# The end of part 1 in another order, and the one-hot of the low rank digits from 16-bit operands

## The chip, the cores and the metric

The kernel runs on one core of a Trainium2 chip. The core has a matrix engine (TensorE, PE in the profile), three engines for element-wise work (VectorE or DVE, ScalarE or ACT, GpSimd or POOL), a synchronisation engine (SyncE or SP) that here only issues DMAs, and 16 DMA engines that move data between the memory outside the core (HBM) and the memory on it (SBUF). Each engine executes its own instructions in a fixed order and waits where an input or a buffer is not ready; an instruction behind a waiting one waits with it.

The metric is the device time of one execution in microseconds (us). It is given as the median of several runs. A profiled execution is a separate one, and it has its own time.

## What is computed

The kernel is one layer of graph attention. There are 3327 nodes with 1024 features, and a symmetric adjacency matrix of integers in which few entries of a row are one.

```python
h = jnp.maximum(_layernorm(x, axis=-1), 0.0)
f = h @ Wf + bf
g = h @ Wg + bg
e = jax.nn.relu(f @ g.T)
scores = jnp.where(adj > 0, e, NEG)
attention = jax.nn.softmax(scores, axis=1)
out = x + attention @ (h @ W + bW)
```

## The kernel before

The kernel doesn't compute the full matrix of scores. It finds the neighbours of each node and gathers only their rows of h. The nodes are held in NT = 26 tiles of 128 rows; the last tile has 127. The code is in `edge_path`, and it has two parts. (A dense way of computing the same stands behind a test at the end, and isn't executed with these inputs.)

**Part 1** makes four things: h, stored in HBM as the table `hd`; the list of neighbours of every row, stored as `pd` with the remaining candidates in `cd`; the matrix A = Wf Wg^T, so that one product per tile yields the vector q with which a row's scores are dot products of q and neighbours' rows of h; and `perm`, the order of all nodes by degree. Part 2 then handles nodes in groups of 128 nodes of like degree.

The main loop of part 1 runs over i from 0 to 22. For tile i+2, `degrees` (line 686, ACT, 691) turns the adjacency into 0 and 1 and adds each row up, and `keys` (695, POOL, 698) multiplies by column numbers, in two halves. For tile i, `segments` (756, DVE, 761) takes the eight largest keys in each of 16 segments, and `listed` (763, DVE, 768 to 776) makes the list out of these 128 candidates. Beside this run the layer norms. `load_x` (678) reads a tile of x. `measured` (700) takes mean and variance on DVE for an odd tile; for an even one, `rooted` (711) takes them with two passes on ACT, and for an odd one it is two short instructions. `inverted` (727, DVE) is a reciprocal, `scaled` (731, ACT) writes h in place, and `store_h` (737) stores it. The tables `at_load`, `at_stats` and `at_scale` (850 to 852) say in which i each tile has these steps. The stage of the loop also issues the load of adjacency tile i+5 (`load_adj`, 671), loads of Wf, and PE's products for A (`plan`). All DMAs of part 1 except three small or late ones go through SP's queue, in the order of the code.

Ranks by degree come from one-hot matrices: `one_hot` (782) makes `oh` from the degrees; `before` and `after` (791, 794) are PE products that add up prefixes; `placed` (797, DVE) reads the row's place off. After the loop comes the tail, lines 965 to 1120, for the last three tiles 23, 24 (`late`) and 25 (`last`). It completes prefix sums, computes `rank`, splits it in a low part of seven bits and a high part (`lo`, `hi`), makes a one-hot of each (`ohp`, line 1034, 3328 elements a partition; `ohs`, 1040), and PE multiplies the two in 26 products (1049). Their result, after three short steps, is `perm` (1057). Two gathers (1062) then fetch the rows of h for the first two groups, and PE computes their q in six products of a third each (1075). DVE meanwhile finishes the lists of tiles 23, 24 and 25 (1096 to 1106).

All of part 1 lies in a `manual_schedule`: each engine has its instructions in the order of the code. Buffers are taken in turn: six of 128 x 1024 for x (`ln`, `xt`), which also receive the two gathers, and five of 128 x 3327 for the adjacency (`kpool`, `r`), which also hold the work space and `ohp` of the tail. A load into a buffer waits for the last reader of what was in it. W is read by one DMA of POOL's queue (1064) into the buffer of Wg's transpose.

**Part 2** has 26 groups. For each, POOL issues gathers of the lists (L), of the group's own rows (H) and of the neighbours' rows (G) into 26 row buffers; PE turns the own rows and computes q; DVE takes a dot product for each neighbour (1222); ACT takes exponentials; the weighted rows are added up on DVE (1272) or PE (1260), and PE multiplies by W (1287). The whole order of instructions comes from `planned` (550), which works it out from assumed durations and start times; once built, it is fixed for each engine. One of its steps, `told` (1318), copies a flag from a PE result that stands behind the last of the six q products (1155); it has its place in DVE's order among the dots of the first group.

Of the kernel before, what the change touches and what calls it, by code (L numbers as in the profile page):

```python
# [10 lines left out]
FP = mybir.dt.float32  # L11
I32 = mybir.dt.int32
AF = mybir.ActivationFunctionType
ALU = mybir.AluOpType
# [7 lines left out]
BF = mybir.dt.bfloat16  # L22
SEG = 16
# [552 lines left out]
def edge_path(ctx: ExitStack, tc: tile.TileContext, x, adj, Wf, bf, Wg, bg, W, bW, out, flag):  # L576
# [11 lines left out]
    nc = tc.nc  # L588
    N, D = x.shape
# [54 lines left out]
    with ExitStack() as part1:  # L644
# [26 lines left out]
        def load_adj(t, parts=((0, N),)):  # L671
            n = rows(t)
            r = rs[t] = kpool.tile([P, N], FP, name="r")
            for c0, c1_ in parts:
                for b, m in pieces(t):
                    nc.sync.dma_start(r.bitcast(I32)[b : b + m, c0:c1_], adj[t * P + b : t * P + b + m, c0:c1_])

        def load_x(t):
            xt = xs[t] = ln.tile([P, D], FP, name="xt")
            for b, m in pieces(t):  # L680
                nc.sync.dma_start(xt[b : b + m], x[t * P + b : t * P + b + m, :])
# [45 lines left out]
        def inverted(t):  # L727
            rstd = stats[t][1]
            nc.vector.reciprocal(rstd[: rows(t)], rstd[: rows(t)])
# [76 lines left out]
        def empty():  # L806
            while emptied1:
                emptied1.pop(0)()
# [40 lines left out]

        at_load = {t: t + 2 for t in range(18)} | {18: 20, 19: 21, 20: 21, 21: 22, 22: 22, 23: 22, 24: 22}  # L850
        at_stats = {t: t + 4 for t in range(16)} | {16: 20, 17: 20, 18: 21, 19: 22, 20: 22}
        at_scale = {t: t + 5 for t in range(16)} | {16: 21, 17: 21, 18: 22}
        of = lambda table, i: [t for t in range(NT) if table.get(t) == i]

        with tc.manual_schedule(engines={
# [5 lines left out]
            for b, e in HALVES:  # L861
                nc.gpsimd.iota(
                    iotaj[:, b:e], pattern=[[1, e - b]], base=b + 1, channel_multiplier=0, allow_small_or_imprecise_dtypes=True
                )
            held = p_c.tile([P, NBIN + BATCH * KL + SEG * 8], FP, name="held")
            iotad, pos = held[:, :NBIN], held[:, NBIN + BATCH * KL :]
# [48 lines left out]
            for i in range(NT - 3):  # L915
                degrees(i + 2)
                keys(i + 2, nc.gpsimd)
                if i < 3:
                    for c in (2 * i + 2, 2 * i + 3):
                        transposed(WgT[:, :, c * P : (c + 1) * P], A_sb[:, c, :D])  # L920
                        empty()
# [15 lines left out]
                if i + 5 < NT:  # L937
                    load_adj(i + 5)
                for c in range(KD):
                    if wants[c] - 2 == i:  # L940
                        load_w(Wf, c)
# [21 lines left out]
                for t in of(at_load, i):  # L963
                    load_x(t) if t >= NT - 3 else None
            late, last = NT - 2, NT - 1
            degrees(last)
            keys(last, nc.gpsimd)
            empty()
            one_hot(late, last)
            one_hot(last, NT)  # L970
            for t in (NT - 7, NT - 6):
                inverted(t)
                scaled(t)
            store_left(NT - 4)
            store_h(NT - 7)
            load_x(last)
            store_h(NT - 6)
            measured(NT - 5, True)
            rooted(NT - 5)
            measured(NT - 4, False)  # L980
            rooted(NT - 4)

            s = 0
            after(counted - 1)
            for t in range(counted, NT):
                before(t)
                segments(NT - 3, s, s + 2)
                s += 2
                placed(t)
                after(t)  # L990
                if t == NT - 3:
                    for u in (NT - 5, NT - 4):
                        inverted(u)
                    for u in (NT - 5, NT - 4):
                        scaled(u)
                        store_h(u)
            segments(NT - 3, s, s + 1)
            measured(NT - 3, True)
            rooted(NT - 3)
            measured(late, False)  # L1000
            rooted(late)

            work = kpool.tile([P, N], FP, name="r")
# [7 lines left out]
            slots = slots.rearrange("p (t s) -> p t s", s=NT)  # L1011
            ohp = kpool.tile([P, N], FP, name="r").bitcast(BF)[:, : NT * P].rearrange("p (t d) -> p t d", d=P)

# [3 lines left out]
            nc.vector.tensor_mul(above, oh, incl[:, None, :].to_broadcast([P, NT, NBIN]))  # L1017
            inverted(NT - 3)
            scaled(NT - 3)
            store_h(NT - 3)  # L1020
            rank = c1.tile([P, NT], FP, name="rank")
            nc.vector.tensor_reduce(rank, above, AX.X, ALU.add)
            ranki = c1.tile([P, NT], I32, name="ranki")
            nc.vector.tensor_add(ranki, rank, rp)
            lo = c1.tile([P, NT], I32, name="lo")
            nc.vector.tensor_scalar(lo, ranki, P - 1, None, op0=ALU.bitwise_and)
            hi = c1.tile([P, NT], I32, name="hi")
            nc.vector.tensor_scalar(hi, ranki, 7, None, op0=ALU.logical_shift_right)
            inverted(late)
            scaled(late)  # L1030
            store_h(late)
            measured(last, True)
            rooted(last)
            nc.vector.tensor_tensor(
                ohp, lo[:, :, None].to_broadcast([P, NT, P]), iotap[:, None, :].to_broadcast([P, NT, P]), op=ALU.is_equal
            )
            inverted(last)
            scaled(last)
            store_h(last)
            nc.vector.tensor_tensor(  # L1040
# [3 lines left out]
                place[:, :, 0, :], ohs, iotap[:, :NT, None].to_broadcast([P, NT, NT]), op=ALU.mult  # L1044
            )
            nc.vector.tensor_scalar(place[:, :, 1, :], ohs, part, None, op0=ALU.mult)
            ps = p_mm.tile([P, CB], FP, name="ps_A")
            for t in range(NT):
                nc.tensor.matmul(
                    ps[:, : 2 * NT], ohp[:, t, :], place[:, t, :, :].rearrange("p a s -> p (a s)"),  # L1050
                    start=(t == 0), stop=(t == NT - 1),
                )
            segments(NT - 3, s + 1, SEG)
            tens = c1.tile([P, NT], FP, name="tens")
# [5 lines left out]
            for s in ORDER[:2]:  # L1060
                hps.append(ln.tile([P, D], FP, name="xt"))
                gather(hps[-1], hd[:, :], perm[:, s : s + 1])
            W_sb = wgpool.tile([P, KD, QW], FP, tag="wg", name="W_sb")[:, :, :O]
            nc.gpsimd.dma_start(W_sb, W.rearrange("(k p) o -> p k o", p=P))

# [29 lines left out]

            listed(NT - 3)
            store_lists(NT - 2 - BATCH, NT - 2)
# [274 lines left out]
```

## Time and profile before

| what | value |
|---|---|
| median of 3 runs | 1243.84 us (1241.71 to 1244.11) |
| the profiled execution's own time | 1279.55 us |
| its span | 1277.8 us |
| mean granted PE clock | 0.951 |
| DVE busy | 1134.0 us (89%) |
| PE busy | 1127.0 us (88%) |
| POOL busy | 876.2 us (69%) |
| ACT busy | 618.1 us (48%) |
| DMA | 374.46 MB, mean 293 GB/s |

The profile is of one execution, and its span is 36 us above the median of the runs; sums over its durations are to be set against its own time. The columns of a slice row are 40 equal parts of the span, and each digit is the busy share in tenths. In a timeline, the bracket behind an instruction says how long its engine sat idle before it and which instruction or DMA seems to have released it. The releaser is inferred; where an instruction awaits several things, it can be the wrong one.

In the stretch around the change the windows of the trace give:

| stretch, us | PE busy | DVE busy | ACT busy | POOL busy | DMA share | GB/s |
|---|---|---|---|---|---|---|
| 140 to 180 | 37.62 | 31.96 | 32.63 | 38.93 | 1.03 | 391 |
| 180 to 200 | 7.81 | 17.75 | 15.86 | 11.45 | 0.96 | 287 |
| 200 to 220 | 1.39 | 12.65 | 18.79 | 10.62 | 0.56 | 193 |
| 220 to 240 | 10.96 | 19.45 | 5.62 | 3.02 | 0.67 | 212 |
| 240 to 250 | 10.00 | 6.77 | 1.87 | 0.00 | 0.86 | 338 |
| 250 to 260 | 10.00 | 3.45 | 1.78 | 7.45 | 0.47 | 140 |
| 400 to 600 | 180.58 | 185.72 | 102.14 | 141.87 | 0.90 | 314 |

### The profile page before, as it was taken

How to read it: one execution, taken by the hardware profiler on the slowest of the kernel's cores; microseconds unless marked ns; L12 is line 12 of the kernel's file. 1: busy time of each engine (PE TensorE's matmuls, PEld its weight loads, DVE VectorE, ACT ScalarE, POOL GpSimd, SP SyncE). 2: the span in 40 equal slices, each digit the busy share in tenths (PEclk: the TensorE clock that was granted, in tenths of full speed). 3: DMA queues.
4: the chain of work that ended last, by engine and by line, in shares of the span. 5: the costliest groups of instructions: out<-in, count | busy, mean ns of one | idle time of the engine just before them, and what ended most of it. 6: DMA issues, size and time to landing. Idle time of an engine off the chain costs nothing. (4 is left out here: it accounts for less than half of the span.)

```text
span 1277.8 us, 14478 instructions
## 1 busy us (share of the span) xinstructions
PE 1127.0 (88%) x4632; PEld 720.7 (56%) x4632; DVE 1134.0 (89%) x2167; ACT 618.1 (48%) x941; POOL 876.2 (69%) x677
## 2 busy tenths in 40 slices
PE   2799980887987899997999799999999999999995
PEld 2566650555646467655766465665655665555553
DVE  6999977778798999999999979898999999999991
ACT  5899978234418256544644254453323433333250
POOL 8999975277576667677677657557676776766711
PEclk9899985798998999999999899999999999989998
DMA  9999996689768989989899879679987998989941
GB/s 369 418 379 397 404 347 233 209 313 340 268 204 298 340 274 328 313 311 311 284 325 293 305 221 332 216 259 330 311 299 236 339 270 305 271 291 296 321 110 52
DMA packets 101803, 374.46 MB, mean 293 GB/s; under 512 B 14747, under 2 KB 18490, under 8 KB 98519
## 3 DMA queue, kind: packets, MB, share of 16 engines
q0 software_dynamic: 80624, 290.96, 67.9%
q1 hardware_dynamic: 21094, 82.49, 17.1%
q8 instruction: 38, 0.62, 0.2%
q14 instruction: 47, 0.39, 0.1%
HBM read 344.11 MB, written 29.30 MB: 292 GB/s over the span
## 5 line engine op out<-in xcount | busy, mean ns | idle before, releaser
L635 POOL DMA_INDIRECT G<-hd,ps x454 | 524.3, 1155 | 243.6 <-issue 103.1
L1222 DVE CUSTOM_DVE_ANT_0 junk<-G,q 128x1024 bf16<-128x1024 f32 x468 | 601.6, 1286 | 40.0 <-DMA G<-hd,ps 28.7
L1209 PE MATMUL p_q<-A_sb,hT 128*128 128x342 f32 x1152 | 361.1, 463 | 14.7 <-ACT hT L1205 5.2
L1287 PE MATMUL p_o<-W_sb,yT 128*128 128x512 f32 x832 | 368.2, 598 | 3.7 <-ACT yT L1283 3.3
L1272 DVE SCALAR_TENSOR_TENSOR G<-G,sc 128x1024 f32<-128x1024 f32 x257 | 330.9, 1287 | 11.5 <-ACT G L1245 10.4
L1209 PEld LDWEIGHTS p_q<-A_sb,hT 128*128 128x128 f32 x1152 | 217.5, 195 | 124.0 <-issue 17.4
L1287 PEld LDWEIGHTS p_o<-W_sb,yT 128*128 128x128 f32 x832 | 158.2, 192 | 194.3 <-issue 184.7
L1260 PE MATMUL p_y<-ident,G 128*128 128x128 f32 x1688 | 208.2, 276 | 21.4 <-issue 11.5
L1260 PEld LDWEIGHTS p_y<-ident,G 128*128 128x128 f32 x1688 | 192.5, 143 | 53.5 <-issue 25.5
L1256 ACT ACTIVATE G<-G,sc 128x1024 f32<-128x1024 f32 x185 | 197.2, 1137 | 0.1
L698 POOL TENSOR_TENSOR r<-r,iotaj 128x1664 f32<-128x1664 f32 (+3 forms) x50 | 183.8, 3762 | 15.0 <-ACT r L691 15.0
L1298 ACT ACTIVATE xp<-p_o,rs 128x512 f32<-128x512 f32 x50 | 33.1, 682 | 213.1 <-DMA out_dram<-xp,perm 80.9
L831 PE MATMUL ps_A<-WgT,WfT 128*128 128x342 f32 x432 | 132.2, 465 | 2.4 <-ACT WfT L826 2.4
L761 DVE MAX8 cand<-r 128x8 f32<-128x208 f32 (+2 forms) x416 | 119.1, 360 | 4.0 <-POOL r L698 3.7
L831 PEld LDWEIGHTS ps_A<-WgT,WfT 128*128 128x128 f32 x432 | 82.5, 195 | 43.5 <-issue 3.3
L1215 ACT COPY q<-p_q 128x342 f32<-128x342 f32 x72 | 31.8, 445 | 128.0 <-PE p_q L1209 51.5
L691 ACT ACTIVATE r<-r 128x3327 f32<-128x3327 int32 (+3 forms) x27 | 77.3, 2862 | 8.1 <-DMA r<-in_adj_dram 8.1
L1283 ACT COPY yT<-p_y 128x512 f32<-128x512 f32 x52 | 29.9, 585 | 75.6 <-remote 43.9
L1205 ACT COPY hT<-p_t 128x512 f32<-128x512 f32 x48 | 27.4, 587 | 67.7 <-PE p_q L1209 32.4
L635 POOL DMA_INDIRECT xp<-in_x_dram,perm x25 | 41.5, 1660 | 22.1 <-ACT xp L1298 15.0
L1202 PE MATMUL p_t<-ident,G 128*128 128x128 f32 x192 | 31.7, 289 | 24.6 <-ACT hT L1205 9.1
L1305 POOL DMA_INDIRECT out_dram<-xp,perm x25 | 31.0, 1239 | 30.3 <-DMA xp<-in_x_dram,perm 22.9
(139 smaller groups left out, 687.2 us busy)
## 6 DMA issues: line engine op xcount, KB each, us to landing
r<-in_adj_dram SPq DMA_DIRECT2D x24, 1663.5 KB, 13.2
xt<-in_x_dram SPq DMA_DIRECT2D x25, 512.0 KB, 13.5
hd<-xt SPq DMA_DIRECT2D x25, 512.0 KB, 10.5
G<-hd,ps POOLq DMA_INDIRECT x454
A_sb<-in_L_gnn_Wg_dram SPq DMA_DIRECT2D x8, 512.0 KB, 17.4
A_sb<-in_L_gnn_Wf_dram SPq DMA_DIRECT2D x8, 512.0 KB, 12.1
W_sb<-in_L_gnn_W_dram POOLq DMA_DIRECT2D x1, 4096.0 KB
cd<-cand SPq DMA_DIRECT2D x25, 64.0 KB, 12.5
```

The lines of the kernel that those rows point to most:

```text
L635: return nc.gpsimd.indirect_dma_start(out=to, out_offset=None, in_=table, in_offset=bass.IndirectOffsetOnAxis(ap=idx, axis=0), **kw,)
L691: nc.scalar.activation(r[:n, b:e], a[:n, b:e], AF.Sign, accum_out=to)
L698: eng.tensor_mul(r[:n, b:e], r[:n, b:e], iotaj[:n, b:e])
L761: nc.vector.max(cands[t][:n, s * 8 : s * 8 + 8], r[:n, s * SW : min(N, (s + 1) * SW)])
L831: nc.tensor.matmul(ps[:, :QB], WfTs[c][:, k, :], WgT[:, k, o : o + QB], start=(k == 0), stop=(k == KD - 1))
L1209: nc.tensor.matmul(ps_q[(3 * t + i) % 2][:, :QB], hT[:, k, :], A_sb[:, k, i * QB : (i + 1) * QB], start=False, stop=(k == KD - 1), skip_gr ...
L1222: nc.vector.tensor_tensor_reduce(junk, row(t, k), q[:, :D], 1.0, q[:, D : D + 1], op0=ALU.mult, op1=ALU.add, accum_out=scs[t % 3][:, k : k ...
L1256: nc.scalar.activation(g, g, AF.Copy, scale=scs[t % 3][:, k : k + 1])
L1260: nc.tensor.matmul(ps_y[g][:, c, :], of[:, (4 * g + c) * P : (4 * g + c + 1) * P], ident, is_transpose=True, start=((t, g) not in begun an ...
L1272: nc.vector.scalar_tensor_tensor(y, row(t, k), scs[t % 3][:, k : k + 1], y, op0=ALU.mult, op1=ALU.add)
L1287: nc.tensor.matmul(ps_o[o], yT[:, k, :], W_sb[:, k, o * CB : (o + 1) * CB], start=False, stop=(k == KD - 1), skip_group_check=True,)
L1298: nc.scalar.activation(to, ps_o[o], AF.Copy, scale=rss[t % 3])
```

## The change

It has three parts; part 2 and the planner are not touched.

1. **Order of the tail.** The tables of the loop are shortened at their ends: statistics of tile 17 move from i = 20 to 21 and those of tile 18 from 21 to 22, and all later tiles' steps to the tail. Tiles 19, 20 and 21 of x are loaded at i = 21 in one block into a buffer of the adjacency pool (`spare`). `degrees` and `keys` of the last tile move into the loop at i = 22. In the tail, four segments of tile 23 are taken between two `placed` steps instead of two, so that all 16 are done before the ranks; the norms of tiles 19 to 25 are spread over the steps of the ranks. The work space and `ohp` thereby come to use the next buffers of the pool, and the two gathers other buffers of `ln`.
2. **W.** Its one DMA on POOL's queue becomes eight of 512 KB on SP's queue: two at the start of the tail, four between the stores of h, and two behind them.
3. **The one-hot of the low digits.** A constant `iotaq` of 128 x 26 bf16 elements a partition is made by POOL at the start; `lo` is also copied to bf16 (`lob`); `ohp` has the tile as its innermost dimension, and its two operands and its result are bf16. The 26 products read their weights from it at a step of 26 elements. `listed` of tile 23 moves ahead of the three steps to `perm`.

The diff, cut to what the prediction speaks of:

```diff
-            xt = xs[t] = ln.tile([P, D], FP, name="xt")
+            if t not in xs:
+                xs[t] = ln.tile([P, D], FP, name="xt")
+            xt = xs[t]
...
-        at_load = {t: t + 2 for t in range(18)} | {18: 20, 19: 21, 20: 21, 21: 22, 22: 22, 23: 22, 24: 22}
-        at_stats = {t: t + 4 for t in range(16)} | {16: 20, 17: 20, 18: 21, 19: 22, 20: 22}
-        at_scale = {t: t + 5 for t in range(16)} | {16: 21, 17: 21, 18: 22}
+        at_load = {t: t + 2 for t in range(18)} | {18: 20, 22: 21, 23: 21, 24: 22}
+        at_stats = {t: t + 4 for t in range(16)} | {16: 20, 17: 21, 18: 22}
+        at_scale = {t: t + 5 for t in range(16)} | {16: 21, 17: 22}
...
+            iotaq = c1.tile([P, P, NT], BF, name="iotaq")
+            nc.gpsimd.iota(
+                iotaq, pattern=[[1, P], [0, NT]], base=0, channel_multiplier=0, allow_small_or_imprecise_dtypes=True
+            )
...
+                if i == NT - 4:
+                    degrees(NT - 1)
+                    keys(NT - 1, nc.gpsimd)
...
+                if i == NT - 5:
+                    spare = kpool.tile([P, N], FP, name="r")
+                    for u in range(NT - 7, NT - 4):
+                        xs[u] = spare[:, (u - NT + 7) * D : (u - NT + 8) * D]
+                        load_x(u)
...
+            W_sb = wgpool.tile([P, KD, QW], FP, tag="wg", name="W_sb")[:, :, :O]
+
+            def load_W(k):
+                nc.sync.dma_start(W_sb[:, k, :], W[k * P : (k + 1) * P, :])
+
             late, last = NT - 2, NT - 1
-            degrees(last)
-            keys(last, nc.gpsimd)
             empty()
+            load_x(last)
+            for k in range(2):
+                load_W(k)
             one_hot(late, last)
             one_hot(last, NT)
...
+            measured(19, True)
+            rooted(19)
+            inverted(18)
             s = 0
             after(counted - 1)
             for t in range(counted, NT):
                 before(t)
-                segments(NT - 3, s, s + 2)
-                s += 2
+                segments(NT - 3, s, s + 4)
+                s += 4
                 placed(t)
                 after(t)
...
+                if t == NT - 4:
+                    inverted(19)
+                    measured(21, True)
+            scaled(18)
+            store_left(NT - 4)
+            store_h(18)
+            scaled(19)
+            store_h(19)
+            load_W(2)
+            measured(20, False)
+            rooted(20)
+            rooted(21)
...
-            ohp = kpool.tile([P, N], FP, name="r").bitcast(BF)[:, : NT * P].rearrange("p (t d) -> p t d", d=P)
+            ohp = kpool.tile([P, N], FP, name="r").bitcast(BF)[:, : NT * P].rearrange("p (d t) -> p d t", t=NT)
...
+            lob = c1.tile([P, NT], BF, name="lob")
+            nc.vector.tensor_copy(lob, lo)
+            measured(22, False)
+            rooted(22)
+            rooted(23)
...
+            inverted(22)
+            scaled(22)
+            store_h(22)
+            load_W(4)
+            inverted(23)
+            scaled(23)
+            store_h(23)
+            load_W(5)
             nc.vector.tensor_scalar(place[:, :, 1, :], ohs, part, None, op0=ALU.mult)
+            measured(last, True)
+            measured(late, False)
+            rooted(late)
+            rooted(last)
             ps = p_mm.tile([P, CB], FP, name="ps_A")
+            nc.vector.tensor_tensor(
+                ohp, lob[:, None, :].to_broadcast([P, P, NT]), iotaq, op=ALU.is_equal
+            )
             for t in range(NT):
                 nc.tensor.matmul(
-                    ps[:, : 2 * NT], ohp[:, t, :], place[:, t, :, :].rearrange("p a s -> p (a s)"),
+                    ps[:, : 2 * NT], ohp[:, :, t], place[:, t, :, :].rearrange("p a s -> p (a s)"),
                     start=(t == 0), stop=(t == NT - 1),
                 )
-            segments(NT - 3, s + 1, SEG)
+            inverted(late)
+            scaled(late)
+            store_h(late)
+            inverted(last)
+            scaled(last)
+            store_h(last)
+            for k in range(6, KD):
+                load_W(k)
+            listed(NT - 3)
...
-            W_sb = wgpool.tile([P, KD, QW], FP, tag="wg", name="W_sb")[:, :, :O]
-            nc.gpsimd.dma_start(W_sb, W.rearrange("(k p) o -> p k o", p=P))
```

More of the change, by code (lines that the diff above doesn't have):

```diff
@@ L964, in edge_path @@
                     load_x(t) if t >= NT - 3 else None
+            W_sb = wgpool.tile([P, KD, QW], FP, tag="wg", name="W_sb")[:, :, :O]
+            def load_W(k):
+                nc.sync.dma_start(W_sb[:, k, :], W[k * P : (k + 1) * P, :])
             late, last = NT - 2, NT - 1
-            degrees(last)
-            keys(last, nc.gpsimd)
             empty()
+            load_x(last)
+            for k in range(2):
+                load_W(k)
             one_hot(late, last)
             one_hot(last, NT)
[L971 to L981, printed above, removed]
+            measured(19, True)
+            rooted(19)
+            inverted(18)
             s = 0
@@ L986, in edge_path @@
                 before(t)
-                segments(NT - 3, s, s + 2)
-                s += 2
+                segments(NT - 3, s, s + 4)
+                s += 4
                 placed(t)
                 after(t)
[L991 to L1001, printed above, removed]
+                if t == NT - 4:
[10 more added lines that the diff above has]
+            rooted(21)
             work = kpool.tile([P, N], FP, name="r")
@@ L1017, in edge_path @@
             nc.vector.tensor_mul(above, oh, incl[:, None, :].to_broadcast([P, NT, NBIN]))
-            inverted(NT - 3)
-            scaled(NT - 3)
-            store_h(NT - 3)
+            inverted(20)
+            scaled(20)
+            store_h(20)
+            inverted(21)
+            scaled(21)
+            store_h(21)
+            load_W(3)
+            measured(23, True)
             rank = c1.tile([P, NT], FP, name="rank")
@@ L1024, in edge_path @@
             nc.vector.tensor_add(ranki, rank, rp)
+            hi = c1.tile([P, NT], I32, name="hi")
+            nc.vector.tensor_scalar(hi, ranki, 7, None, op0=ALU.logical_shift_right)
             lo = c1.tile([P, NT], I32, name="lo")
             nc.vector.tensor_scalar(lo, ranki, P - 1, None, op0=ALU.bitwise_and)
[L1027 to L1039, printed above, removed]
+            lob = c1.tile([P, NT], BF, name="lob")
[3 more added lines that the diff above has]
+            rooted(23)
             nc.vector.tensor_tensor(
@@ L1094, in edge_path @@
                     pq.append(bank(j + 1, False))
-            listed(NT - 3)
             store_lists(NT - 2 - BATCH, NT - 2)
```

## The prediction, made before the changed kernel was run

> **What bounds the kernel now.** I read the page first, for where the idle time is.
>
> ```profile
> PE   2799980887987899997999799999999999999995
> DVE  6999977778798999999999979898999999999991
> ACT  5899978234418256544644254453323433333250
> POOL 8999975277576667677677657557676776766711
> DMA  9999996689768989989899879679987998989941
> ```
>
> A slice is 31.9 us. From the ninth slice on (255 us) DVE is nearly full, then PE too; in slices 6 to 8 (160 to 255 us), the tail of part 1, no engine is. Whatever moves the start of part 2 should move its end, because part 2's order on ACT, DVE, PE and POOL is a fixed list that starts when its inputs are there. So the question is when those inputs arrive. The timelines of DVE and ACT over 165 to 225 us show the waits in the tail (columns: start, us, engine, line, what; in brackets the idle time before it and its releaser).
>
> ```profile
> 180.98 1.29 DVE L707 BATCH_NORM_STATS2 st<-xt 128x6 f32<-128x512 f32 x2 [7.38 <-DMA xt<-in_x_dram]
> ...
> 204.88 0.21 DVE L784 TENSOR_TENSOR oh<-held,pay 127x48 bf16<-127x48 f32 x1 [3.46 <-ACT r L691]
> ...
> 211.40 0.16 DVE L729 RECIPROCAL rstd<-rstd 128x1 f32<-128x1 f32 x1 [2.71 <-ACT rstd L725]
> ...
> 219.88 3.57 DVE L1034 TENSOR_TENSOR r<-lo,iotap 128x3328 bf16<-128x3328 int32 x1
> ```
> ```profile
> 182.54 0.20 ACT L716 ACTIVATE nmr<-mv 128x1 f32<-128x1 f32 x1 [6.67 <-DVE mv L709]
> ...
> 201.80 2.96 ACT L691 ACTIVATE r<-r 127x3327 f32<-127x3327 int32 x1
> ```
>
> DVE waits for x of tile 17; ACT stands behind it with the degrees of tile 23; the degrees of tile 25 come so late that the one-hot at 204.88 waits for them. With 0.57, 0.69 and 0.33 of short waits DVE idles 15.1 us between 173.6 and 243.9. The timelines of POOL and PE then show the two chains that leave the tail:
>
> ```profile
> 229.43 1.08 POOL L635 DMA_INDIRECT xt<-hd,perm  x1 [17.16 <-DVE held L772]
> ...
> 250.42 1.01 POOL L635 DMA_INDIRECT ps<-pd,perm  x1 [17.67 <-DMA cd<-cand]
> ```
> ```profile
> 235.02 1.94 PE L815 MATMUL ps_tr<-ident,xt 128*128 128x128 f32 x8 [3.50 <-DMA xt<-hd,perm]
> ...
> 245.20 23.16 PE L1075 MATMUL ps_A<-A_sb,WfT 128*128 128x342 f32 x80
> ```
>
> Chain Q: last h in HBM, gather of h (229.43), PE's q products, q of the first tile at 255.06 (254.61 plus the 0.45 of L1092), last product at 268.36. The gather's named releaser is a DVE step; perm was ready at 227.94, so I take the last store of h (issued 225.15 to 225.95) as what it awaited. Chain L: last list stored, first gather of lists at 250.42, rows, first dot at 258.62.
>
> [...]
>
> **The change, part by part.**
>
> *Start.* The new iota of 3328 elements takes about the 3.00 us that L862's 3327 took, on POOL at 4.66. Behind it are memset(deg), so ACT's first degrees (5.71) start near 7.7, and DVE's first keys and maxima about 2 us later; DVE waited 1.81 before 19.94 anyway, which covers it. Behind it too is the copy of bgT, 13.26 to 16.3; keys(1) starts about 0.25 late, and POOL's own gap of 1.01 at 39.25 takes that back. Cost 0; at twice the duration about 2.3 us, as POOL's keys then run without a gap to 178.9.
>
> *Stages 20 to 22.* measured(17) moves one stage later, past listed(20) and segments(21). DVE goes on at 173.6: listed and placed 2.2, segments(21) 4.65, so 180.5, and x of tile 17 lands at 180.98: 0.5 left of 7.38. ACT does degrees(23) at 175.9 rather than 182.84; degrees(24) at 182.9; degrees(25), now in this loop, at about 187 to 190.1, when the last adjacency tile lands. Then scaled(17) and rooted(18) to 195.3. DVE: measured(17) 1.45, listed(21), placed and one-hot 3.4, segments(22) 4.5, listed and placed 2.7: 193.0. POOL's keys chain from 179.0 at 7.37 a tile; keys(23) is done at 186.4, in time. The x tiles 19 to 21 go to a free adjacency buffer, so their loads need not wait for stores of h.
>
> *Tail.* DVE: one-hots 0.3, measured(19) 1.43, wait for rooted(18), at 195.4. Four rounds of four maxima (0.283 each) and a hit (0.12), 5.0, plus measured(21) and a reciprocal 1.5: 201.9. About 0.4 of wait for PE's last prefix product, new because no bn_stats lies there. Scan to product 1.85, reciprocals 0.2, measured(23) 1.43, reduce 1.49, ranks, digits and the new cast 0.55, two one-hot products 1.7: 209.5. Now ACT is late: rooted(22) at 2.85 ends 210.05, rooted(23) 210.35; wait 0.85. Place 0.35, measured(25) 1.43: 212.3. One-hot of the low digits 1.8 [...]: 214.1. The next reciprocal waits for ACT's two scaled tiles (1.45 each) and rooted(24), rooted(25): 216.45. So the faster one-hot buys nothing here: with 3.6 DVE would still be waiting. Its 26 products (1.31[...]) run beside this and listed(23), 2.35. perm at 219.4, against 227.94.
>
> *Chain L.* The rest of DVE (both last tiles) took 230.20 to 243.87; now 219.4 to 233.1. The stores landed 6.55 later with W's 4 MB saturating the DMA (409 GB/s at 242 to 244); without it I take 5, bounds 4 and 6.55: lists gathered at 238.1, 12.3 earlier, first row at 246.3.
>
> *Chain Q.* Last scaled ends at 219.3 (225.12 before); plus the same 4.3 to the gather: 223.6, 5.8 earlier. q of the first tile 249.3, last product 262.6. All of SP's queue counts: W goes ahead of h in six pieces of 512 KB, two later. From 180 to 232 the windows add up to 11.3 MB; now 14.2 MB must be through by 223, or 330 GB/s. The windows show 340 to 412 when loads and stores run, but 178 to 248 at 180 to 186. It just fits.
>
> *Part 2.* First dot at 249.4, 9.2 earlier, now set by q. After six dots DVE executes the flag's copy (L1319), which awaits PE's last product: 262.8, a new wait of about 5 us with six dots behind it. These then find their rows landed: six at 1.33, tile 0 done at 271, against 280.06: 9 earlier. Rows lead by 12.3, and DVE waited 18.6 us for rows between 256 and 400, so part may be won back. I take 9.7 of the 9 to 12.3.
>
> Against the profiled execution's 1279.55 that is 1269.9. The median of 1243.84 is 2.8% lower; I scale by it, 9.7 x 0.972 = 9.4: 1234.4.
>
> **The rivals.**
>
> 1. *Half the lead* (1239.5). If the 7.38 us wait is partly the profiler's, or bWb's load, whose buffer now is that of the second gathered h tile (its transposes end near 240), stands before the last list stores in SP's queue: lists at about 243.8, 6.6 earlier, less what rows then cost. For it: bWb went ahead of them in before (238.06).
> 2. *No change* (1243.8). The lead is eaten by part 2's fixed order. Against it: DVE is starved early, not late.
> 3. *Slower* (1249). W's pieces delay the last h. From 180 on, below 14.2 MB/49.4 us = 288 GB/s, h lands after 229.4 and chain Q turns later than before. At 260 GB/s: 234.6, 5.2 late; the flag's wait passes it to all dots. For it: 233 and 209 GB/s in slices 7 and 8; against it: these slices had nothing to move.
> 4. *The new one-hot is not read twice as fast.* 1.8 us on DVE, hidden; 1234.4 stays.
>
> **How the numbers follow.** What the measurement can tell from no change is 0.2%, 2.5 us. Forecast 0.60 (case 4 in it), half the lead 0.15, no change 0.09, slower 0.16. Faster 0.75. The forecast's own range is 1230 to 1238 (12.3 with more won back; 6 by chain Q alone). The range goes to 1245, leaving most of the slower case out, and down to 1229.
>
> **What would show it.** DVE's wait before the statistics of tile 17 under 1 us; degrees(25) by 191; perm near 219; gather of h near 224 and of lists near 238; a wait of some 5 us at the flag; the new one-hot at 1.9 us, followed by a DVE wait for rooted(24). Wrong if h lands after 229, if keys(1) starts after 17.5, or if DVE's waits after 300 us grow by what the tail won.

## The result, and the profile after

The changed kernel took 1234.16 us (median of 6 runs, 1229.64 to 1236.07) against 1243.62 for the kernel before on the same chip: a ratio of 0.9919, 95% interval 0.9899 to 0.9939, or 9.5 us less. The forecast was 1234.4. The profiled execution took 1234.97 us (span 1233.1). The first profile of the kernel before, 36 us above its own median, can't be held against it as a whole. A second one (first experiment) has both chains 2.7 us earlier than the first, as the changed kernel's second has them 1.7 and 2.6 earlier; so first profiles are set against first ones here, and second against second ones below.

The rows of slices, now 30.8 us each:

```profile
PE   2799990699988899998999999999998999999995
DVE  5999998759998999999999999999999999999991
ACT  5899987326518346534644355453433233333260
POOL 9999995275676776777776777557767776777711
DMA  9999999698778998989998998879988999899932
```

The stretch in which no compute engine is full is now slices 7 and 8 (185 to 247 us), and DMA is fuller in slices 6 to 8 (9, 9, 6) than before (9, 6, 6). The timelines of DVE and of ACT in the tail (columns as before: start, us, engine, line, what, in brackets the idle time before it and its releaser):

```profile
181.23 1.29 DVE L709 BATCH_NORM_STATS2 st<-xt 128x6 f32<-128x512 f32 x2 [0.64 <-DMA xt<-in_x_dram]
...
212.17 0.44 DVE L731 RECIPROCAL rstd<-rstd 128x1 f32<-128x1 f32 x2 [0.77 <-ACT rstd L727]
...
214.27 1.84 DVE L1070 TENSOR_TENSOR r<-lob,iotaq 128x3328 bf16<-128x3328 bf16 x1
...
218.31 0.44 DVE L731 RECIPROCAL rstd<-rstd 128x1 f32<-128x1 f32 x2 [2.21 <-ACT rstd L727]
...
221.44 0.18 DVE L1090 TENSOR_SCALAR perm<-tens 128x26 int32<-128x26 f32 x1
```
```profile
189.55 2.98 ACT L693 ACTIVATE r<-r 127x3327 f32<-127x3327 int32 x1 [3.41 <-DMA r<-in_adj_dram]
```

The reader sees the wait of 7.38 us for x of tile 17 shrunk to 0.64 (5.43 to 0.52 between the second profiles), the one-hot at half its former 3.57 us, and right behind it a wait of 2.21 us for ACT: what the one-hot saved, DVE waits. ACT's degrees of the last tile wait for the adjacency to land. The two chains that leave the tail, by the timelines of POOL and PE:

```profile
227.06 1.07 POOL L635 DMA_INDIRECT xt<-hd,perm  x1 [24.09 <-DMA W_sb<-in_L_gnn_W_dram]
...
238.03 0.99 POOL L635 DMA_INDIRECT ps<-pd,perm  x1 [8.63 <-DMA cd<-cand]
```
```profile
233.76 1.94 PE L817 MATMUL ps_tr<-ident,xt 128*128 128x128 f32 x8 [10.62 <-DMA xt<-hd,perm]
...
243.98 23.17 PE L1106 MATMUL ps_A<-A_sb,WfT 128*128 128x342 f32 x80
```

| step, us | before | forecast | after |
|---|---|---|---|
| DVE's wait before the statistics of tile 17 | 7.38 | under 1 | 0.64 |
| degrees of tile 25 end | 204.8 | 190.1 | 192.5 |
| perm ready | 227.94 | 219.4 | 221.62 |
| gather of h (chain Q) | 229.43 | 223.6 | 227.06 |
| first dot | 258.62 | 249.4 | 253.86 |
| last q product ends | 268.36 | 262.6 | 267.15 |
| gather of lists (chain L) | 250.42 | 238.1 | 238.03 |
| DVE's wait at the flag | none | 5 | 5.50 |

Chain L came as forecast, 12.4 us earlier. Chain Q came only 1.2 earlier instead of 5.8. Yet the total is right, so the experiments ask how a start that is 1.2 us earlier on one chain and 12.4 on the other makes 9.5.

### The profile page after: what moved, and what is told of

Same layout as the page of the kernel before. It is cut to its first block, busy times and chain, and to the rows that moved or that the text cites. A ratio compares the mean times of both kernels' runs of the same rounds, so it can differ in the third digit from the quotient of the medians.

```text
span 1233.1 us, 14492 instructions
## 1 busy us (share of the span) xinstructions
PE 1112.3 (90%) x4632; PEld 712.4 (58%) x4632; DVE 1131.3 (92%) x2168; ACT 617.3 (50%) x941; POOL 876.6 (71%) x677
## 5 line engine op out<-in xcount | busy, mean ns | idle before, releaser
L1239 PE MATMUL p_q<-A_sb,hT 128*128 128x342 f32 x1152 | 353.2, 456 | 3.1 <-ACT p_q L1248 2.4
L1239 PEld LDWEIGHTS p_q<-A_sb,hT 128*128 128x128 f32 x1152 | 214.0, 192 | 107.8 <-issue 10.0
L1271 ACT ACTIVATE sc<-sc,nm 128x10 f32<-128x10 f32 (+10 forms) x36 | 11.0, 305 | 113.7 <-DVE nm L1261 99.1
L635 POOL DMA_INDIRECT xp<-in_x_dram,perm x25 | 40.3, 1610 | 21.4 <-ACT xp L1328 14.4
```

The costliest lines, as they stand in the source:

```text
L635: return nc.gpsimd.indirect_dma_start(out=to, out_offset=None, in_=table, in_offset=bass.IndirectOffsetOnAxis(ap=idx, axis=0), **kw,)
L1239: nc.tensor.matmul(ps_q[(3 * t + i) % 2][:, :QB], hT[:, k, :], A_sb[:, k, i * QB : (i + 1) * QB], start=False, stop=(k == KD - 1), skip_gr ...
```

## The experiments

In the diffs below a minus is a line of the changed kernel, unless another kernel is named. "Dot 20" is the twenty-first of part 2's 468 dots on DVE (the first being dot 0); its start, and that of the last dot, are read from DVE's timeline. The changed kernel was run again beside the second group of experiments (medians of these: before 1241.69); the last group ran beside a kernel before of 1241.16. The chip of the W and one-hot experiments gave the kernel before a median of 1267.93 with 1256 to 1283, and the changed kernel was not run on it, so there the profiles tell more than the times.

**The kernel before, a second profile.** No edit.

> The kernel before, profiled a second time. My reading is that its first profile, 36 us above its median, was slow only in part 2. Then this one has a span near 1240 us, the first gather of lists near 250, dot 20 near 299 and, from dot 20 to the last dot, about 903 us as the changed kernel has, against 937 in the first profile. Rival: part 2 of the kernel before is really slower dot by dot (rows that come late, later contention), so that the gap to the changed kernel goes on growing after dot 20; then the 937 comes back.

It took 1240.44 us. Its gather of lists, last q products and dot 20, and then the same of the changed kernel's second profile:

```profile
247.68 1.01 POOL L635 DMA_INDIRECT ps<-pd,perm  x1 [17.75 <-DMA cd<-cand]
```
```profile
242.47 23.17 PE L1075 MATMUL ps_A<-A_sb,WfT 128*128 128x342 f32 x80
```
```profile
295.44 1.29 DVE L1222 CUSTOM_DVE_ANT_0 junk<-G,q 128x1024 bf16<-128x1024 f32 x1
```
```profile
236.35 0.99 POOL L635 DMA_INDIRECT ps<-pd,perm  x1 [8.15 <-DMA cd<-cand]
```
```profile
241.37 23.17 PE L1106 MATMUL ps_A<-A_sb,WfT 128*128 128x342 f32 x80
```
```profile
287.01 1.30 DVE L1252 CUSTOM_DVE_ANT_0 junk<-G,q 128x1024 bf16<-128x1024 f32 x1 [1.62 <-ACT q L1245]
```

From dot 20 (295.44) to the last dot (1198.09) are 902.7 us; the changed kernel has 903.2 in its first profile and 903.0 in its second. So part 2 runs at much the same pace in both kernels after dot 20, the 937 us belonged to that one execution, and 8.4 us of the gain are made ahead of dot 20. Two limits of this: in the profiles of the variants below, away from the noisier chip, the same stretch takes 900.8 to 906.3 us, so differences of that size in it can't be given to an edit; and the medians gain 9.5 and 10.3 us, 1 to 2 more than dot 20, which no profile places.

**The changed kernel again, and one without the wait at the flag.** The second kernel takes the flag from one partition's count, so it leaves out the test of all other rows:

```diff
-            nc.vector.tensor_copy(flag[0:1, 0:1], ps_y[1][0:1, 0, 0:1])
+            nc.vector.tensor_copy(flag[0:1, 0:1], bads[0:1, 0:1])
```

> The changed kernel once more, on the chip of the runs that follow, so that they can be compared with it; the first four experiments ran on a chip whose kernel before had a median of 1267.93. If the gain doesn't depend on the chip: 0.992 of the kernel before. If it is smaller there, 0.995 as with the one-hot of before or W on POOL's queue.

> The changed kernel with the flag copied from the tests of one partition in SBUF, not from PE's product over all partitions; it leaves out the test of the other rows. DVE's wait of 5.5 us ahead of the seventh dot goes, and the dots 7 to 12 come about 5 us earlier. If chain Q and the flag set the end, 5 us (0.4%) faster than the changed kernel. If the lead of the rows sets it and the wait is won back, within 1.5 us of it.

The changed kernel took 1231.38 us (ratio 0.9919, 0.9901 to 0.9938), the one without the wait 1232.01 (0.9932, 0.9911 to 0.9953): no gain. The waits of DVE between 256 and 400 us (columns: what waited, for what, us in all, times, longest), first of the second profile of the kernel before, then of the changed kernel, then without the flag's wait:

```profile
DVE junk L1222 <- DMA G<-hd,ps: 16.0, 13, 4.8
```
```profile
DVE flag L1349 <- PE p_y L1185: 5.5, 1, 5.5
DVE junk L1252 <- DMA G<-hd,ps: 4.5, 7, 1.3
DVE junk L1252 <- ACT q L1245: 1.6, 1, 1.6
DVE rs L1282 <- ACT sc L1271: 0.5, 1, 0.5
```
```profile
DVE junk L1252 <- ACT q L1245: 4.5, 1, 4.5
DVE rs L1282 <- ACT sc L1271: 2.6, 1, 2.6
DVE junk L1252 <- DMA G<-hd,ps: 2.5, 3, 1.1
```

Before, DVE waited for rows: 16.0 us. Now it waits for q. Without the flag's wait the six dots go on at once and DVE waits at dot 20 for the copy of the next q: 4.45 us instead of 1.62, and 2.61 instead of 0.46 at a reciprocal that ACT releases. Dot 20 starts at 287.26 against 287.01. The wait at the flag is a place where DVE waits for PE, not a cost of its own.

**Each chain delayed by itself.** Chain L: thirty maxima of 0.3 us, made a second and third time, ahead of the last list. Chain Q: six products of 512 columns, overwritten afterwards, ahead of the first q product.

```diff
             segments(last, 0, SEG)
+            segments(last, 1, SEG)
+            segments(last, 1, SEG)
             listed(last)
```
```diff
             pq.append(bank(0, True))
+            for _ in range(6):
+                nc.tensor.matmul(pq[3], ident, A_sb[:, 0, :CB], start=True, stop=True)
+            nc.scalar.copy(pq[3][:, :QB], vb[:, :QB])
             third(pq[0], hTs[0], 0)
```

> The changed kernel with 30 redundant maxima on DVE ahead of the last tile's list: chain L about 8.5 us later (first gather of lists near 246.5), chain Q as it was. If the lead of the rows sets the end, 6 to 8.5 us (0.5 to 0.7%) slower than the changed kernel, most of its gain. If chain Q sets it (first dot at 253.9 after q, flag at 267.3), at most 1 us slower, since the first row then lands near 255.

> The changed kernel with six redundant products of 512 columns on PE ahead of the first q product: chain Q about 5.5 us later (last q product near 272.7), chain L as it was. If chain Q sets the end, 5.5 us (0.45%) slower than the changed kernel. If the lead of the rows does, within 1.5 us of it, as the dots then find more rows landed.

With the lists late: 1238.84 us (0.997, 0.9957 to 0.9983), 7.5 above the changed kernel. The lists were gathered at 246.04 (9.7 later), the waits for rows came back, and dot 20 started at 295.52, 8.5 later. DVE's waits, 256 to 400 us:

```profile
DVE junk L1254 <- DMA G<-hd,ps: 17.2, 15, 3.4
DVE rs L1284 <- ACT sc L1273: 0.5, 1, 0.5
```

With q late: 1238.61 us (0.9982, 0.9969 to 0.9995), 7.2 above, with a spread of 1232 to 1244. Its profiled execution (1234.91) shows the added products and the q products behind them:

```profile
235.83 5.42 PE L1118 MATMUL ps_A<-A_sb,ident 128*128 128x512 f32 x12 [0.54 <-ACT ps_A L1101]
241.09 4.76 PE L1106 MATMUL ps_A<-A_sb,WfT 128*128 128x342 f32 x16
...
246.56 23.16 PE L1106 MATMUL ps_A<-A_sb,WfT 128*128 128x342 f32 x80
```

The last q product ends at 269.72, 5.2 later, and dot 20 starts 5.2 later. That a delay of 5.2 made 7.2 in the median but 3.2 in the profiled execution is not explained; behind dot 20 that execution was 2.1 us quicker than the changed kernel's second profile (900.8). Both chains carry the gain, then: delay either, and most of it is gone.

That suggests a rule. In the profiles of all chips but the noisier one, dot 20 starts close to the later of two times: the last q product's end plus 22.5 us (PE's fills and the next tile's transposes and q, which dot 20 awaits), or the gather of the first lists plus 47.8 to 49.5 us (POOL then issues a gather every 1.25 to 1.3 us at its quickest, and the dots ahead of dot 20 wait for their rows). The first constant holds to 0.1 us in six of the rows; the second is a fit to the rows "before" and "lists late", and 48.5 lies in the middle. The rule was read from the rows between; the first row and the last three were measured after it. The first profile of the kernel before fits it too (250.4 plus 48.5 against 299.2). On the noisier chip the kernel before with the new one-hot fits (248.6 plus 48.5 against 297.7), and W behind the stores doesn't: it comes 3.9 us after the later of the two. The other two kernels of that chip had pauses of PE or ACT, told below.

| kernel | last q product ends | + 22.5 | lists gathered | + 48.5 | dot 20 |
|---|---|---|---|---|---|
| before, second profile | 265.6 | 288.1 | 247.7 | 296.2 | 295.4 |
| changed, first profile | 267.2 | 289.7 | 238.0 | 286.5 | 289.6 |
| changed, second profile | 264.5 | 287.0 | 236.4 | 284.9 | 287.0 |
| no wait at the flag | 265.4 | 287.9 | 237.0 | 285.5 | 287.3 |
| lists late | 265.4 | 287.9 | 246.0 | 294.5 | 295.5 |
| q late | 269.7 | 292.2 | 236.5 | 285.0 | 292.2 |
| iota late | 267.8 | 290.3 | 239.5 | 288.0 | 290.2 |
| PE kept warm | 262.0 | 284.5 | 236.7 | 285.2 | 284.5 |
| both | 266.3 | 288.8 | 239.7 | 288.2 | 288.8 |

By the rule the kernel before was held by L, with Q 8 us ahead of it. The change took 11 to 12 us off L and 1.1 to 1.2 off Q, so that now Q holds: 296.2 to 287.0 by the rule, 295.4 to 287.0 measured. The last dot starts 8.1 us earlier (1198.09 to 1189.96), so in these profiles what was won at dot 20 stays to the end.

**W.** All eight pieces behind the last store of h; and W as one DMA on POOL's queue, as before.

```diff
-            for k in range(2):
-                load_W(k)
...
-            for k in range(6, KD):
+            for k in range(KD):
                 load_W(k)
```
```diff
                 gather(hps[-1], hd[:, :], perm[:, s : s + 1])
+            nc.gpsimd.dma_start(W_sb, W.rearrange("(k p) o -> p k o", p=P))
```

The first also drops the four single pieces between the stores, the second all of `load_W`'s calls.

> The changed kernel with all eight pieces of W behind the last store of h. If the six pieces ahead of h are what made chain Q late (it began its gather of h at 227.06 where 223.6 was reckoned), the gather starts near 224, the wait at the flag's copy falls from 5.5 us to about 2, and the sixth dot and those behind it come some 3 us earlier; if that is passed to the end, the median is about 1231. If the end is set by the lead of the gathered rows (chain L, first gather of lists at 238.03) and chain Q's lateness is won back later, the median stays at 1234, within 2.

> The changed kernel with W read as before, by one DMA of POOL's queue behind the two gathers of h. Gather of h near 224, as with W last; the last list stores then share the DMA engines with W's 4 MB, so the first gather of lists comes 6.5 us rather than 2.9 us after the last list is made, near 241.7. If chain L sets the end: about 3.5 us slower than the changed kernel, 1238. If chain Q does: about 3 us faster, 1231. If moving W was worth nothing either way: 1234.

Behind the stores: 1263.89 us (0.9976, 0.995 to 1.0001). The gather of h went out at 224.33, as forecast for a queue without W ahead, but h then landed 8.1 us later, with W's eight pieces issued just ahead of it (with W behind the gather, on POOL's queue, it took 4.8, and in the changed kernel 5.9):

```profile
224.33 1.07 POOL L635 DMA_INDIRECT xt<-hd,perm  x1 [21.30 <-issue]
...
241.66 0.96 POOL L635 DMA_INDIRECT ps<-pd,perm  x1 [14.98 <-PE ps_tr L817]
```
```profile
232.44 1.94 PE L817 MATMUL ps_tr<-ident,xt 128*128 128x128 f32 x8 [12.09 <-DMA xt<-hd,perm]
```

The last q product ended at 264.48, where the changed kernel's second profile has 264.54, and the lists were gathered 5.3 later than there. From perm to the gather are 4.3 us here and 4.4 with W on POOL's queue, and 5.0 to 5.9 in the profiles with W pieces ahead of h: those pieces cost the gather 0.6 to 1.6 us, and pieces just behind the stores cost the landing as much and the lists more. On POOL's queue: 1262.92 us (0.9955, 0.9928 to 0.9982), gather of h at 224.80, lists at 241.12. Its profiled execution (1273.98, 11 us above its median) had idle stretches of ACT and PE between 266 and 284 us whose cause the profile doesn't name, and the changed kernel has no time on this chip, so how much of the gain comes from W's place is open. That the lists come 3 to 5 us later in both is shown, and where: the last list is made at 233.7 and 234.1, as in the changed kernel (233.6), but takes 8.0 and 7.1 us to the gather, where that has 2.8. So of the 11 to 12 us off L, W's place carries 3 to 5, and the order of the tail the rest, as the one-hot moves nothing there.

**The one-hot.** The changed kernel with the one-hot of before; and the kernel before with the new one alone.

```diff
-                ohp, lob[:, None, :].to_broadcast([P, P, NT]), iotaq, op=ALU.is_equal
+                ohp, lo[:, :, None].to_broadcast([P, NT, P]), iotap[:, None, :].to_broadcast([P, NT, P]), op=ALU.is_equal
...
-                    ps[:, : 2 * NT], ohp[:, :, t], place[:, t, :, :].rearrange("p a s -> p (a s)"),
+                    ps[:, : 2 * NT], ohp[:, t, :], place[:, t, :, :].rearrange("p a s -> p (a s)"),
```

`iotaq` and `lob` go with it. The second kernel makes the reverse edit in the kernel before.

> The changed kernel with the one-hot of the low digits as it was before, and without the new constant and the cast. The prediction has the faster one-hot hidden: the reciprocal behind it waited 2.21 us for ACT in the changed kernel, so with 3.57 us instead of 1.84 this wait falls to about 0.5 and perm stays within 0.3 of 221.6; POOL's first keys go back from 19.06 to 16.2. Median 1234, within 2. Rival: the 1.7 us are passed on, 1236; or the 5.25 us of the constant at the start cost more than the one-hot gains, and this is faster, 1231.

> The kernel before with the new one-hot alone (constant, cast, layout). There the one-hot stands ahead of the last reciprocal, and so ahead of the last store of h and of perm: both about 1.6 us earlier, at the start 2.9 us later keys that DVE takes up before the tail. Median about 1242 (1.6 less than before). Rival: POOL's later keys reach the tail, which is bound there, and it is 1 to 2 us slower, 1245.

With the old one: 1260.67 us (0.9952, 0.993 to 0.9975). Its DVE timeline:

```profile
212.43 3.57 DVE L1064 TENSOR_TENSOR r<-lo,iotap 128x3328 bf16<-128x3328 int32 x1
...
216.47 0.44 DVE L731 RECIPROCAL rstd<-rstd 128x1 f32<-128x1 f32 x2 [0.47 <-ACT rstd L727]
...
219.60 0.18 DVE L1084 TENSOR_SCALAR perm<-tens 128x26 int32<-128x26 f32 x1
```

The wait behind the one-hot is 0.47 instead of 2.21: the 1.73 us that the new form saves DVE stands there again. perm comes at 219.78, against 219.93 in the changed kernel's second profile. This rests on the tail alone: further on, PE's q products were broken by pauses that the profile gives no cause for, and the first dot came at 269.06, so the rest of this profile can't be compared. The times can't tell a small gain of the one-hot from none, either, as the changed kernel was not run on this chip.

In the kernel before, where no such wait follows, the new one alone gave 1268.92 us (1.0015, 0.9985 to 1.0045), a time from which 1.6 us can't be read. Its profile shows them: the degrees of the last tile and the lists, then the degrees in the kernel before's second profile, whose lists are above:

```profile
201.22 2.96 ACT L691 ACTIVATE r<-r 127x3327 f32<-127x3327 int32 x1
```
```profile
248.57 1.01 POOL L635 DMA_INDIRECT ps<-pd,perm  x1 [17.92 <-DMA cd<-cand]
```
```profile
198.99 2.96 ACT L691 ACTIVATE r<-r 127x3327 f32<-127x3327 int32 x1
```

From the end of the degrees to the gather of lists it is 44.4 us with the new one-hot and 45.7 in both profiles of the kernel before. So there the new form shortened the tail by 1.3 us, near the 1.6 expected; in the changed kernel the wait for ACT takes this away.

**Could the limits be moved further?** The new iota behind POOL's last keys, instead of at the start; PE kept busy while it waits for h; both.

```diff
-            nc.gpsimd.iota(
-                iotaq, pattern=[[1, P], [0, NT]], base=0, channel_multiplier=0, allow_small_or_imprecise_dtypes=True
-            )
...
                     keys(NT - 1, nc.gpsimd)
+                    nc.gpsimd.iota(
+                        iotaq, pattern=[[1, P], [0, NT]], base=0, channel_multiplier=0, allow_small_or_imprecise_dtypes=True
+                    )
```
```diff
+            pq.append(bank(0, True))
+            for _ in range(8):
+                nc.tensor.matmul(pq[3], ident, A_sb[:, 0, :CB], start=True, stop=True)
+            nc.scalar.copy(pq[3][:, :QB], vb[:, :QB])
             transposed(hTs[0], hps[0])
             empty()
-            pq.append(bank(0, True))
```

> The changed kernel with the new iota moved from the start of POOL's work to behind its last keys, where POOL is idle. My theory, that the tail of part 1 stands behind POOL's chain of keys: the first degrees of ACT start near 7.2, keys(1) near 16.2, all keys end near 200.5 instead of 203, perm near 219.5, both chains 1.9 us earlier, and the kernel 1.5 to 2 us faster than the changed kernel (about 1229.5 where that has 1231.4). Rival, as I predicted: the later start costs nothing; then no change.

> The changed kernel, with eight products of 512 columns that are overwritten put on PE while it waits for the first gathered h, and one bank filled ahead of it. If chain Q sets the start and PE's low clock after its idle time costs some 3 us in it: the first transposes take near 1 us for eight instead of 1.94, the last q product ends about 3 us earlier (near 261.5), dot 20 starts 2 to 3 us earlier, and the kernel is 2 to 2.5 us faster than the changed kernel. Rival, that q was never the limit (the row gathers are): the q products end earlier and the time stays.

> Both together: with the rule that dot 20 starts at the later of the last q product's end plus 22.5 us and the first gather of lists plus 49 us, q ends near 259.6 and the lists are gathered near 234.5, so 283.5 by the lists against 282.1 by q: lists decide, and the kernel is about 3.5 us faster than the changed kernel. If the two gains add up in full: 4 to 4.5. If neither chain is the limit any more: 2 or less.

*Iota late:* 1236.18 us (0.9952, 0.9933 to 0.9971). My expectation failed in its sign. POOL's keys did end 2.1 us earlier, at 200.85, but nothing in the tail waits for them: the scan of the ranks starts at 202.32, and at 201.86 in the changed kernel, because ACT's last degrees await the adjacency in both. And DVE lost 3.1 us. POOL and DVE of this kernel, then DVE's same instruction in the first profile of the changed kernel:

```profile
182.47 18.38 POOL L700 TENSOR_TENSOR r<-r,iotaj 128x1663 f32<-128x1663 f32 x5
200.76 5.28 POOL L924 IOTA iotaq<- 128x3328 bf16 x1
```
```profile
202.61 3.47 DVE L1027 TENSOR_SCALAR incl<-incl 128x48 f32<-128x48 f32 x1
```
```profile
204.45 0.19 DVE L1027 TENSOR_SCALAR incl<-incl 128x48 f32<-128x48 f32 x1
```

An instruction on 48 elements took 3.47 us instead of 0.19: it ended at 206.08, when the iota did (206.04). In the changed kernel's second profile the same instruction, started at 202.15 while POOL's keys ran to 202.91, took 0.81 and ended at 202.96. No bracket shows this, because the instruction counts as busy. In these profiles the instruction ended 0.04 and 0.05 us after POOL's work, while the scan just ahead of it, also beside the iota, took 0.25 us, as in the changed kernel's first profile with POOL idle. Why the one ran longer and the other didn't, no run here shows.

*PE kept warm:* 1232.55 us (0.9925, 0.9907 to 0.9943). On PE's timeline the eight added products end at 229.79, and the transposes of the first h now take 1.09 us. The changed kernel has 1.94 for them, in its first profile at a granted clock of 0.50, and there 1.03, at a clock of 1.00, for those of the second h at 243.11:

```profile
222.66 7.13 PE L1116 MATMUL ps_A<-A_sb,ident 128*128 128x512 f32 x16 [0.54 <-ACT ps_A L1101]
231.95 1.09 PE L817 MATMUL ps_tr<-ident,xt 128*128 128x128 f32 x8 [2.16 <-DMA xt<-hd,perm]
233.28 4.87 PE L1106 MATMUL ps_A<-A_sb,WfT 128*128 128x342 f32 x16 [0.24 <-ACT WfT L818]
```

The last q product comes 2.5 earlier (262.03) and dot 20 too (284.49). Yet the kernel was not faster than the changed one: their ratios to the kernel before, 0.9925 and 0.9919, don't differ. DVE's waits for rows from 284 us to the end, of the changed kernel's second profile and of this one:

```profile
DVE junk L1252 <- DMA G<-hd,ps: 8.5, 13, 1.4
```
```profile
DVE junk L1255 <- DMA G<-hd,ps: 10.9, 14, 1.3
```

2.4 us more, as much as q had won. That reading rests on one execution each, with a difference no larger than the spread of this stretch given above, and the intervals leave room for a gain of some 2 us. *Both:* 1234.04 us (0.9939, 0.9922 to 0.9957). DVE's long instruction beside the iota is in it again (3.68 us), and as h landed later PE stood idle for 2.96 us behind its added products, after which the transposes took 1.85. Dot 20 starts at 288.77, and the 3.5 us expected aren't there.

None of these is shown to beat the changed kernel.

## Why the prediction was right

- *The wait for x goes, the degrees come earlier, the one-hot takes half:* right, with 0.64, 192.5 and 1.84 us. The 1.8 for the one-hot was my estimate and rested on no row of the profile before. The degrees ended 2.4 later than forecast (0.1 in the second profile). That the one-hot buys nothing in this tail because ACT is late behind it is shown by the old form in its place (wait of 0.47 instead of 2.21).
- *Start, cost 0:* right in the cost, off in the term. The iota took 5.25 us on POOL, not 3.0, and ACT's first degrees moved by 4.3 us and POOL's first keys by 2.9. POOL's keys then ran without a gap, which the step had only for twice the duration, and keys(1) started at 19.06: one of the three signs of being wrong that the prediction had named ("after 17.5") came true. It did no harm, because nothing waited for the last keys, which ended at 203.
- *Chain L, lists at 238.1:* right, 238.03. The stores landed within 2.85 us of the last list, less than the 5 taken, which made good a list that was 2.1 late: two errors that cancel.
- *Chain Q, 5.8 us earlier:* this is the step that was mis-sized; it was 1.2 (1.1 between the second profiles). Of the 4.55 us by which the last product missed 262.6, 2.2 is the tail (perm 6.3 us earlier instead of 8.5, and 5.2 between the second profiles); 1.25 is the way from perm to the gather of h, where W's pieces stand ahead of the last stores ("it just fits" was 0.6 to 1.6 us too kind, by the W experiment); and 1.1 the way from the gather to the last product, as h took 6.7 us to land instead of 5.6. This last part is not steady: between the second profiles it is 0.3 us shorter, not longer. In the first profile the tail is late because the last adjacency tile landed later (degrees to 192.5 instead of 190.1). In the second they end at 190.2, as forecast, but there the kernel before is earlier too, and its wait for x of tile 17, which was to be won, is 5.43 us instead of 7.38.
- *The flag's wait of about 5:* right, 5.50, but it is not on the path to the end: without it DVE waits for the next q.
- *Part 2, 9.7 of the 9 to 12.3:* right in the sum, and in part by luck. I had the range from Q (9) and L (12.3) and took nearly all from the first dots. The first dot moved only 4.8 (4.7 between the second profiles); the rest, to 8.4 at dot 20, is the waits for rows that vanished, the part for which I had written "part may be won back". The sum came out because the kernel before was held by L, which I had right, and because Q had been 8 us ahead of L, so that moving little it cost little: had it moved 5.8 as forecast, the rule would put dot 20 only 2 to 3 us earlier, where L's limit lies. That also shows the luck: with both chains as forecast (262.6 and 238.1) the rule gives dot 20 at 286.6, some 12.5 us before the 299.2 of the profile forecast from, not 9.7. The forecast valued its own chain times 3 us too low, and chain Q, 4.6 us later than forecast, took these 3 us back.
- *Half the lead:* its mechanism, bWb's load ahead of the last list stores, didn't occur: bWb was issued at 244.17, after them. Its other ground holds in part: 2 of the 7.38 us were not there in the second profile. *Slower:* its turning point, the last h in HBM after 229.4, wasn't reached: the gather that awaits it went out at 227.06, and at 225.86 in the second profile. The third sign of being wrong, longer waits of DVE after 300 us, stayed away too: for rows they are 8.5 us, against 8.9 before, in the second profiles.
- *Slips of the working:* none changes the forecast much. Six pieces of 512 KB are 3.1 MB, which makes 14.4 MB and 335 GB/s rather than 14.2 and 330. The 26 products took 1.94 us, 0.63 more than the 1.31 of before. From the ninth slice on DVE was at 7 to 9 tenths, not nearly full; part of the rest were the waits for rows that the change then removed. And the scaling by 0.972 (0.3 us) has no ground: most of what made that profile long lay behind dot 20 (937 us against 903).

## What to carry to other kernels

Where two chains start a saturated stage, write down each one's arrival and its distance to a common point, and take the later: the gain of an edit is the shift of that maximum, not of either chain, and the next limit is the other chain. A wait that is new in the profile is a cost only if nothing else would have held its engine at the same place; take it out and look before counting it. An engine with idle time isn't always free to take work: with the new iota in POOL's idle time, an instruction of DVE beside it took 3.47 us instead of 0.19.

## What the runs showed that I had not expected

- An instruction of DVE on 48 elements ran 3.47 and 3.68 us beside POOL's iota, and 0.19 us when POOL was idle; the profile shows it as busy time.
- An iota of 3328 bf16 elements with a step of zero innermost took 5.25 us on POOL, where 3327 fp32 elements in two plain runs take 3.00.
- The 26 products that read their weights at a step of 52 bytes took 1.94 us, against 1.31 with adjacent ones: 24 ns more each, hidden here.
- PE ran the eight transposes of the first h in 1.94 us after some 11 us of idle time, but also after 3.50 and 4.17 us in the two profiles of the kernel before; in the first profiles of both kernels the granted clock over them was 0.50. They took 1.09 us after 2.16 us (kept busy till then), and 1.85 after 2.96. So here 3.5 us without work cost as much as 11.
